# A layer planner's odd steps: one VectorE place, and a second one only when a job took a TensorE place

## The chip, the cores and the metric

The kernel runs on one core of a Trainium2 chip. The metric is the device time of one execution in microseconds. Before the change the median of 3 runs is 6233.53 us (6230.06 to 6236.76). Its engines are named as in the profile: PE (TensorE), PEld (its weight loads), DVE (VectorE), ACT (ScalarE), POOL (GpSimd) and SP (the queue that issues nearly all DMAs).

## What is computed

Two layers on x of shape 4 x 128 x 64 x 64, all in float32. The first is attention over the 4096 positions of an image, with a residual and a normalisation over the channels. The second adds a 3 x 3 convolution, a spectral term (a Fourier transform, a channel mix and its inverse) and a Mamba block, whose core is a scan over the positions.

```python
# layer 0, per image, 4 heads of 32 channels
attn = softmax(einsum('bhnd,bhmd->bhnm', Q, K) * scale)
y    = (einsum('bhnm,bhmd->bhnd', attn, V) merged) @ Wo + bo + x_flat
y    = normalised over channels * gamma + beta
# layer 1
xs   = silu(depthwise causal conv of 4 taps over xi + b)      # 256 channels
dt   = softplus(x_dbl[:8] @ dt_proj + b)
h    = exp(dt*A) * h + dt * B * xs                            # 16 states, 4096 positions
out  = spatial conv + spectral term + out_proj((h.C + xs*D) * silu(z))
```

## The kernel before, in words

The 4096 positions of an image are cut into 8 chunks of 512, so there are 32 chunks. Attention works on a chunk and one of two pairs of heads at a time (a half, H, 64 in all), and in each half walks over 32 tiles of 128 keys. One tile is one **step** t of the main loop (L1019 to the end of the function). So there are 2048 steps of attention, and a chunk of 64 steps. I call the steps 64k to 64k+63 **stretch k** and count the steps in it from 0 to 63.

What a step always issues is written out in the loop, in this order:

- `scores_for_exp` (L472): six matmuls per step into the PSUM tile s2 (L480) and an exponential on ACT into e (L488).
- `scores_for_max` (L424): four matmuls for a tile 39 steps ahead into the PSUM tile s1 (L436), and a maximum on DVE (L443). There is one s1, so the four matmuls of a step wait until the maximum of the step before is done.
- In even steps `scan_state` (L808): a scan on DVE (L817), and on POOL a copy of the state (L826), a product with C (L827) and a sum (L846, for the first state L844). In odd steps `scan_decay` on ACT (L801) and `scan_input_term` on POOL (L806, up to the end of attention).
- a call of `plan.step`, which hands out the step's **places** to jobs.
- `times_values` (L491) for the tile of the step before: four matmuls with V (L500). At the last tile of a half the sum is copied to oz on ACT and DVE (L509, L510).

Everything else is done by **jobs**: Python generators that stop at `yield "PB"`, `yield "D"` and so on, and say by it what they need next: P a place on PE, D on DVE, A on ACT, B one of two PSUM banks, f and x a buffer. `Plan.step` (L122) goes once through the jobs, sorted by rank and due time, and lets each job go on whose needs can be met in this step; each place it uses is gone. A job is let go on once per step, but for P: while its next need is P alone and P places are left, it goes on (L146 to L148). Places left from a step before count for nothing, because L125 sets D, P and A anew. The order of the instructions on every engine thus follows from counts of places and banks alone, with no times in it. During attention, even steps have no place on DVE and PE and one on ACT, odd steps have 2 places on each of the three (L1051 to L1056). Before and after attention a step has 4.

The jobs that ask for DVE places, with the lines of what they do there:

- `scan_input(c, hf)` (L660), one for each half of the 256 channels: the 4 taps of the causal convolution (L674 and three times L679; the sum stands in a bank), then a `sigmoid` (L599): L603, L605 and L608 on ACT, L611 on DVE, L613 on ACT, and a product on POOL (L689).
- when both are done `scan_bc` (L695), and then `scan_dt(c, hf)` (L711): a matmul (L714), ACT work from L722 to L734, with the last (L737) together with L738 on DVE, three products on POOL (L739 to L741), and three steps later, on ACT, a scaling of xs by D (L748) that has to wait until L741 has read xs.
- `gate(c)` (L751): a matmul (L757) and a sigmoid for each half, each ended by a product on POOL (L765).
- `project_kv` (L341), only while a next image's keys are still to be made, that is in stretches 0 to 23 (L350, L355, L356), `project_q` (L405: L412, L417, L418), `output_projection` (L543: L556, L564 to L570, then L587) and `scan_output(c)` (L924): two products on POOL (L938) as soon as the gates of the chunk are there, then four matmul records on PE (L948) that read them, and L954 on DVE.

Also named below: `convolve` (L880, matmuls of 9 taps, L891), `spectral` (L850, its last ACT copy is L874), `flips` (L966), which at the ends of images 0 to 2 gives POOL two further additions (L921, L922) in stretches 8 and 9, 16 and 17, 24 and 25, `normalise` (L512, on POOL L533), and `scan_load` (L779), the DMA of a state's B and C (L784), which has three buffers.

Of the kernel before, what the change touches and what calls it, by code (L numbers as in the profile page):

```python
# [17 lines left out]
P = 128  # L18
# [81 lines left out]
class Plan:  # L100
# [18 lines left out]
    def release(self, bank, steps=1):  # L119
        self.freed.append((self.t + steps, bank))  # L120

    def step(self, t, places):  # L122

        self.t = t
        self.places |= places  # L125
        self.free += [bank for when, bank in self.freed if when <= t]
        self.freed = [e for e in self.freed if e[0] > t]
        for e in sorted((e for e in self.later if e[0] <= t), key=lambda e: e[:3]):
            self.jobs.append((e[1], e[0], e[2], Job(e[3])))
            self.later.remove(e)  # L130
        self.jobs = sorted((j for j in self.jobs if not j[3].done), key=lambda j: j[:3])
        kept = 0
        for *_, job in self.jobs:
            bank = None
            if "B" in job.need and len(self.free) <= kept:
                continue
            if any(c != "B" and not self.places[c] for c in job.need):
                kept += "B" in job.need
                continue
            for c in job.need:  # L140
                if c == "B":
                    bank = self.free.pop(0)
                else:
                    self.places[c] -= 1
            job.advance(bank)
            while not job.done and job.need == "P" and self.places["P"]:  # L146
                self.places["P"] -= 1
                job.advance(None)  # L148
        self.jobs = [j for j in self.jobs if not j[3].done]
# [6 lines left out]
def attention_then_conv_mamba(  # L156
# [43 lines left out]
    for h in range(HEADS):  # L200
        k, j = divmod(h, 2)
        c = COL["bk"] + k
# [9 lines left out]
    for h in range(HEADS):  # L212
        k, j = divmod(h, 2)
        c = COL["bq"] + h
# [112 lines left out]
    plan = Plan(2, {"x": 2, "f": 1})  # L327
# [96 lines left out]
    def scores_for_max(H, s):  # L424

        k = H % PAIRS
        m, t = divmod(s, TPC)
        assert have["K", k, m] == H // PAIRS // NCH
        if s == 0:
            part[H] = att.tile([P, TPC, 2, NCH], F32, tag="part", name=f"part_{H}")  # L430

        tag = "s2" if H == 0 and s % 2 else "s1"
        sc = psum.tile([P, 2, L], F32, tag=tag, name=f"s1_{H}_{s}")
        for n in range(2):
            for j in range(2):
                nc.tensor.matmul(  # L436
                    sc[:, j, :],
                    QT[H][rows[j], n, t * P : (t + 1) * P],
                    KK[k][m][rows[j], :],
                    start=n == 0,  # L440
                    stop=n == 1,
                )
        nc.vector.tensor_reduce(part[H][:, t, :, m], sc, AX.X, ALU.max)  # L443
# [28 lines left out]
    def scores_for_exp(H, m):  # L472

        k = H % PAIRS
        i, t = divmod(m, TPC)
        assert have["K", k, i] == H // PAIRS // NCH
        s = psum.tile([P, 2, L], F32, tag="s2", name=f"s2_{H}_{m}")
        for n, mov in enumerate((QT[H][:, 0, :], QT[H][:, 1, :], MX[H])):
            for j in range(2):
                nc.tensor.matmul(  # L480
                    s[:, j, :],
                    sel[rows[j], :] if n == 2 else KK[k][i][rows[j], t * P : (t + 1) * P],
                    mov[rows[j], :],
                    start=n == 0,
                    stop=n == 2,
                )
        e = att.tile([P, 2, L], F32, tag="e", name=f"e_{H}_{m}", bufs=3)
        nc.scalar.activation(e, s, AF.Exp)  # L488
        es[H, m] = e

    def times_values(H, m):  # L491

        k = H % PAIRS
        i, t = divmod(m, TPC)
        assert have["V", i] == H // PAIRS // NCH
        if m == 0:
            po[H] = psum.tile([P, L], F32, tag="o", name=f"po_{H}")
        e = es.pop((H, m))
        for j in range(2):
            nc.tensor.matmul(  # L500
                po[H][used[j], :],
                VA[i][:, t, 2 * k + j, :],
                e[:, j, :],
                start=m == 0,
                stop=m == NT - 1,
            )
        if m == NT - 1:
            p = po.pop(H)
            nc.scalar.activation(oz[k][used[0], :], p[used[0], :], AF.Identity)  # L509
            nc.vector.tensor_copy(oz[k][used[1], :], p[used[1], :])  # L510
# [284 lines left out]
    def scan_decay(c, v):  # L795
        n, hf = divmod(v, NH)
        k = hf * NS + n

        tag = "o" if plan.t >= HALVES * NT + 2 and v % 2 else "dA"
        dA[c, v] = psum.tile([P, L], F32, tag=tag, name=f"dA_{c}_{k}")  # L800
        nc.scalar.activation(dA[c, v], dts[c][hf], AF.Exp, scale=negA[:, k : k + 1])  # L801

    def scan_input_term(c, v, engine):
        n, hf = divmod(v, NH)
        db[c, v] = loc.tile([P, L], F32, tag="db", name=f"db_{c}_{hf * NS + n}")
        engine.tensor_tensor(db[c, v], us[c][hf], bcs[c, n][0], ALU.mult)  # L806

    def scan_state(c, v):  # L808

        n, hf = divmod(v, NH)  # L810
        k = hf * NS + n
        assert (c, hf) in scaled
        if c >= CHUNKS - 2:
            hs = flat(VA[v % 4])
        else:
            hs = loc.tile([P, L], F32, tag="hs", name=f"hs_{c}_{k}")
        nc.vector.tensor_tensor_scan(  # L817
            hs,
            dA.pop((c, v)),
            db.pop((c, v)),  # L820
            state[:, k : k + 1] if c % NCH else zero,
            ALU.mult,
            ALU.add,
        )
        if c % NCH < NCH - 1:
            nc.gpsimd.tensor_copy(state[:, k : k + 1], hs[:, L - 1 :])  # L826
        nc.gpsimd.tensor_tensor(hs, hs, bcs[c, n][1], ALU.mult)  # L827
        if hf == NH - 1 and (c, n) in taken:
            spare.append((plan.t + 6, taken.pop((c, n))))
        elif hf == NH - 1:  # L830
            ring[0] += 1
        if c >= CHUNKS - 2:

            if v == 0:
                late = psum.tile([P, NH, L], F32, tag=f"s{CHUNKS - c}", name=f"acc_{c}")
                for h in range(NH):
                    accs[c, h] = late[:, h, :]
            if n == 0:
                nc.tensor.matmul(accs[c, hf], ident, xss[c][hf], start=True, stop=False)
            nc.tensor.matmul(accs[c, hf], ident, hs, start=False, stop=n == NS - 1)  # L840
        elif n == 0:
            acc = loc.tile([P, L], F32, tag=f"acc{hf}", name=f"acc_{c}_{hf}")
            accs[c, hf] = acc
            nc.gpsimd.tensor_tensor(acc, xss[c][hf], hs, ALU.add)  # L844
        else:
            nc.gpsimd.tensor_tensor(accs[c, hf], accs[c, hf], hs, ALU.add)  # L846
# [170 lines left out]
    t = 6 - SLOT  # L1017
    loaded = 0
    end = (CHUNKS + 3) * SLOT  # L1019
    while t < end or not plan.idle():  # L1020
        H, m = divmod(t, NT)
        if 0 <= H < HALVES:
            scores_for_exp(H, m)
        h1, s1 = divmod(t + LEAD, NT)
        if 0 <= h1 + 1 < HALVES:
            scores_for_max(h1 + 1, s1)
        H, m = divmod(t - 1, NT)
        last = m == NT - 1
        if last and 0 <= H < HALVES:
            times_values(H, m)  # L1030
        c, s = divmod(t - LAG, SLOT)
        odd = s % 2 == 1
        if -1 <= c < CHUNKS:
            v = c * STATES + s // 2
            if not odd:
                if v >= 0:
                    scan_state(*divmod(v, STATES))
            else:
                if 0 <= v + 1 < CHUNKS * STATES:
                    scan_decay(*divmod(v + 1, STATES))  # L1040
                if 0 <= v + 2 < CHUNKS * STATES:
                    late = t > HALVES * NT
                    scan_input_term(
                        *divmod(v + 2, STATES), nc.vector if late else nc.gpsimd
                    )

                if loaded < CHUNKS * NS and loaded // NS in bcds:
                    if ring[0] or spare[0][0] <= t:
                        scan_load(*divmod(loaded, NS))
                        loaded += 1  # L1050
        if t < -LEAD or t > HALVES * NT:  # L1051
            plan.step(t, {"D": 4, "P": 4, "A": 4})
        elif odd:
            plan.step(t, {"D": 2, "P": 2, "A": 2})
        else:
            plan.step(t, {"D": 0, "P": 0, "A": 1})  # L1056
        if not last and 0 <= H < HALVES:
            times_values(H, m)
        t += 1
# [76 lines left out]
```

## Time and profile before

| | before |
|---|---|
| median of 3 runs | 6233.53 us |
| the profiled execution | 6236.14 us |
| its span (first to last instruction) | 6234.4 us |
| granted TensorE clock, mean | 0.982 |
| start of step 0 | 131.4 us |
| start of the last step, 2047 | 5983.5 us |
| DVE L817, scan, in attention | 832 + 128 times, 1275 ns |
| DVE L679, a tap | 192 times, 738 to 746 ns |
| DVE L674, the first tap | 64 times, 807 ns |
| DVE L611 and L738 | 128 + 64 times, 677 and 678 ns |
| ACT L488, the exponential | 2048 times, 1023 ns |
| POOL L806, L827, L846 | 948, 952 and 900 times, 1281, 1277 and 1279 ns |

A step's four matmul records of L480 with Q and K (8192 in all) give its start in the trace. So the start of every step and the length of every stretch can be read off, and a wait is what a step lasts above another step with the same matmuls. Stretch 12, for example, runs from 2300.07 to 2483.62 us, and stretch 27 from 5063.60 to 5250.67 us. Lines in the profile are those of the kernel before.

### The profile page before, as it was taken

The page shows a single profiled execution, that of the slowest core. Times are in us where ns is not written, and L with a number is a line of the kernel's source. Part 1 is how long each engine was busy: PE and PEld are TensorE (multiplying, and loading weights), DVE is VectorE, ACT ScalarE, POOL GpSimd, SP SyncE. Part 2 cuts the span into 40 slices and gives each one's busy share as a digit, 9 for nine tenths or more (in the row PEclk, how much of TensorE's full clock was granted, in tenths as well). Part 3 has the DMA queues.
Part 4 walks back from the last instruction along what each step waited for, and adds up shares of the span by engine and source line. Part 5 has one row for each costly group of instructions (what it writes and reads, how often), then busy time and mean ns, then how long its engine had stood idle before and what let it go on. Part 6 is the DMA issues. An engine that isn't in the chain of part 4 may idle for free. (4 is left out here: it accounts for less than half of the span.)

```text
span 6234.4 us, 83338 instructions
## 1 busy us (share of the span) xinstructions
PE 6005.2 (96%) x32076; PEld 2540.9 (41%) x32076; DVE 4286.5 (69%) x4406; ACT 3585.0 (58%) x4858; POOL 4579.0 (73%) x4819
## 2 busy tenths in 40 slices
PE   5999999999999999999999999999999999999966
PEld 2444444444444444444444444444444444444321
DVE  4556776777777676777667777776777666767647
ACT  1455666565666555666656566665566556556643
POOL 0005887778887777888787888777788777778877
PEclk7999999999999999999999999999999999999987
DMA  3001222223222222222322221122322211112223
GB/s 111 14 25 47 63 56 61 63 64 98 79 71 60 63 65 60 62 63 73 89 82 65 61 65 60 57 64 67 98 66 71 55 54 54 54 55 58 63 80 85
DMA packets 234624, 404.97 MB, mean 65 GB/s; under 512 B 39272, under 2 KB 40816, under 8 KB 234224
## 3 DMA queue, kind: packets, MB, share of 16 engines
q1 hardware_dynamic: 229840, 397.75, 22.6%
q8 instruction: 251, 4.11, 0.3%
q10 hardware_dynamic: 4384, 1.89, 0.1%
q14 instruction: 149, 1.22, 0.1%
HBM read 350.54 MB, written 49.02 MB: 64 GB/s over the span
## 5 line engine op out<-in xcount | busy, mean ns | idle before, releaser
L443 DVE TENSOR_REDUCE part<-s 128x2 f32<-128x1024 f32 x2048 | 2501.7, 1222 | 1627.4 <-PE s L436 1625.9
L488 ACT ACTIVATE e<-s 128x1024 f32<-128x1024 f32 x2048 | 2095.5, 1023 | 2271.7 <-PE s L480 2263.0
L500 PE MATMUL po<-e,V 128*33 128x512 f32 x8192 | 2160.9, 606 | 2.6 <-DVE oz L510 0.3
L480 PE MATMUL s<-Q,K 64*128 64x512 f32 x8192 | 1504.7, 445 | 22.3 <-ACT e L488 18.5
L436 PE MATMUL s<-K,Q 64*128 64x512 f32 x8192 | 1322.2, 400 | 41.2 <-DVE part L443 39.6
L827 POOL TENSOR_TENSOR hs<-hs,bc 128x512 f32<-128x512 f32 x952 | 1215.5, 1277 | 177.5 <-DVE hs L817 108.6
L480 PEld LDWEIGHTS s<-Q,K 64*128 64x128 f32 x8192 | 610.7, 185 | 1748.9 <-ACT e L488 1179.0
L806 POOL TENSOR_TENSOR db<-u,bc 128x512 f32<-128x512 f32 x948 | 1214.8, 1281 | 0.0
L846 POOL TENSOR_TENSOR acc<-acc,hs 128x512 f32<-128x512 f32 x900 | 1150.9, 1279 | 70.5
L817 DVE TENSOR_TENSOR_SCAN hs<-dA,state,db 128x512 f32<-128x512 f32 x832 | 1060.7, 1275 | 86.0 <-ACT dA L801 54.0
L436 PEld LDWEIGHTS s<-K,Q 64*128 64x128 f32 x8192 | 766.3, 186 | 276.7 <-DVE part L443 99.4
L480 PE MATMUL s<-MX,sel 64*128 64x512 f32 x4096 | 810.9, 392 | 0.0
L826 POOL COPY state<-hs 128x1 f32<-128x1 f32 x864 | 160.2, 185 | 844.8 <-DVE hs L817 844.8
L801 ACT ACTIVATE dA<-dt,negA 128x512 f32<-128x512 f32 x1024 | 702.6, 686 | 116.0 <-DVE hs L817 63.6
L500 PEld LDWEIGHTS po<-e,V 128*33 128x33 f32 x8192 | 299.3, 109 | 913.8 <-issue 879.7
L480 PEld LDWEIGHTS s<-MX,sel 64*128 64x128 f32 x4096 | 384.6, 185 | 92.6
L891 PE MATMUL pf<-xp,cw 128*128 128x512 f32 x576 | 288.2, 617 | 0.0
L452 POOL COPY wide<-mx 128x128 f32<-128x128 f32 x256 | 63.4, 294 | 200.7 <-DVE mx L449 200.7
L817 DVE TENSOR_TENSOR_SCAN hs<-dA,zero,db 128x512 f32<-128x512 f32 x128 | 163.2, 1275 | 7.7 <-POOL db L806 7.4
L840 PE MATMUL acc<-V,cst 128*128 128x512 f32 x128 | 90.1, 807 | 78.2 <-POOL V L827 78.0
L533 POOL TENSOR_TENSOR oz<-oz,rz 128x512 f32<-128x512 f32 x64 | 81.9, 1280 | 107.1 <-DMA rz<-rd 107.1
L891 PEld LDWEIGHTS pf<-xp,cw 128*128 128x128 f32 x576 | 96.2, 188 | 132.4 <-issue 127.4
(144 smaller groups left out, 3847.8 us busy)
## 6 DMA issues: line engine op xcount, KB each, us to landing
bc<-bcd SPq DMA_DIRECT2D x487, 512.0 KB
K<-kd SPq DMA_DIRECT2D x64, 256.0 KB
rz<-rd SPq DMA_DIRECT2D x128, 128.0 KB
K<-bcd SPq DMA_DIRECT2D x42, 256.0 KB
vd<-vst SPq DMA_DIRECT2D x32, 264.0 KB
V<-vd SPq DMA_DIRECT2D x32, 264.0 KB
xq<-in_x SPq DMA_DIRECT2D x32, 256.0 KB
xk<-in_x SPq DMA_DIRECT2D x32, 256.0 KB
```

Source lines behind the costliest of these rows:

```text
L436: nc.tensor.matmul(sc[:, j, :], QT[H][rows[j], n, t * P : (t + 1) * P], KK[k][m][rows[j], :], start=n == 0, stop=n == 1,)
L443: nc.vector.tensor_reduce(part[H][:, t, :, m], sc, AX.X, ALU.max)
L480: nc.tensor.matmul(s[:, j, :], sel[rows[j], :] if n == 2 else KK[k][i][rows[j], t * P : (t + 1) * P], mov[rows[j], :], start=n == 0, stop= ...
L488: nc.scalar.activation(e, s, AF.Exp)
L500: nc.tensor.matmul(po[H][used[j], :], VA[i][:, t, 2 * k + j, :], e[:, j, :], start=m == 0, stop=m == NT - 1,)
L801: nc.scalar.activation(dA[c, v], dts[c][hf], AF.Exp, scale=negA[:, k : k + 1])
L806: engine.tensor_tensor(db[c, v], us[c][hf], bcs[c, n][0], ALU.mult)
L817: nc.vector.tensor_tensor_scan(hs, dA.pop((c, v)), db.pop((c, v)), state[:, k : k + 1] if c % NCH else zero, ALU.mult, ALU.add,)
L826: nc.gpsimd.tensor_copy(state[:, k : k + 1], hs[:, L - 1 :])
L827: nc.gpsimd.tensor_tensor(hs, hs, bcs[c, n][1], ALU.mult)
L846: nc.gpsimd.tensor_tensor(accs[c, hf], accs[c, hf], hs, ALU.add)
L891: nc.tensor.matmul(pf, cw[:, k, :], xps[c][:, dy : dy + RPC, dx : dx + W], start=k == 0, stop=False)
```

## The change

In an odd step of attention there is one place on DVE in place of two. The first job in that step that takes a place on PE by its own turn (not by the inner loop for further P) adds one place on DVE, which jobs that come later in the same pass can take. Places on PE and ACT, even steps, and the steps before and after attention stay as they are. No instruction is added or taken away: jobs only get their places in other steps.

```diff
-    def step(self, t, places):
+    def step(self, t, places, more=False):
         self.t = t
+        self.more = more
         self.places |= places
...
                 else:
                     self.places[c] -= 1
+                    self.places["D"] += (c == "P") * self.more
+                    self.more &= c != "P"
             job.advance(bank)
...
         elif odd:
-            plan.step(t, {"D": 2, "P": 2, "A": 2})
+            plan.step(t, {"D": 1, "P": 2, "A": 2}, more=True)
         else:
             plan.step(t, {"D": 0, "P": 0, "A": 1})
```

## The prediction, made before the changed kernel was run

> **What bounds the kernel now.** I read the page first, then the waits, then stretches of equal content against each other.
>
> ```profile
> PE 6005.2 (96%) x32076; PEld 2540.9 (41%) x32076; DVE 4286.5 (69%) x4406; ACT 3585.0 (58%) x4858; POOL 4579.0 (73%) x4819
> ...
> L443 DVE TENSOR_REDUCE part<-s 128x2 f32<-128x1024 f32 x2048 | 2501.7, 1222 | 1627.4 <-PE s L436 1625.9
> ...
> L436 PE MATMUL s<-K,Q 64*128 64x512 f32 x8192 | 1322.2, 400 | 41.2 <-DVE part L443 39.6
> ```
>
> PE is the bound; its waits for the maximum on DVE are small (41.2 us before L436). But a busy share is a mean. Attention lasts from 131.4 to 5983.5 us. Adding up, step by step, what each step lasts above the quarter-lowest step with the same matmuls gives 119 us of waits in it. They do not lie evenly. Stretches 4 to 23 last 183.6 us nearly all (of it 2.2 us waits), whereas stretch 3 has 7.2 us of waits and stretches 25 to 31 have 7.6, 5.9, four times 7.2 to 7.3, and 8.6. Busy times of whole stretch 12 and its steps 0 to 20, then of stretch 27 and its steps 0 to 20 (columns: window, its length, PE, PEld, DVE, ACT, POOL):
>
> ```profile
> core 0: us, PE busy (x) PEld busy (x) DVE busy (x) ACT busy (x) POOL busy (x), PEclk, DMA share, GB/s
> 2300.07:2483.62 183.55, 182.90 (x1000) 78.14 (x998) 131.48 (x135) 111.44 (x152) 146.79 (x157) 1.00 0.22 61
> 2300.07:2355.59 55.52, 54.91 (x324) 24.43 (x322) 42.31 (x50) 39.31 (x55) 48.95 (x52) 1.00 0.22 62
> 5063.60:5250.67 187.07, 182.53 (x990) 76.17 (x989) 131.16 (x135) 111.45 (x151) 147.16 (x157) 1.00 0.20 55
> 5063.60:5123.06 59.46, 55.54 (x325) 24.26 (x324) 43.59 (x52) 37.44 (x50) 53.80 (x57) 1.00 0.21 59
> ```
>
> Steps 0 to 20 have the same PE jobs in both, but last 59.46 us in stretch 27 against 55.52: 3.94 us more, all of it waiting. The timeline shows a typical cause, at step 6 of stretch 27, where a step loses 1.49 us:
>
> ```profile
> 5079.56 1.28 POOL L741 TENSOR_TENSOR u<-dt,xs 128x512 f32<-128x512 f32 x1
> ...
> 5080.87 0.72 ACT L748 ACTIVATE xs<-xs,vec 128x512 f32<-128x512 f32 x1 [1.19 <-POOL u L741]
> ...
> 5081.50 1.00 ACT L488 ACTIVATE e<-s 128x1024 f32<-128x1024 f32 x1
> ```
>
> In stretches 3 and 26 to 31 both scan_dt halves end in step 1, on the two DVE places of one step. That puts six products (L739 to L741) on POOL at once. ACT's in-order queue then stands before L748 until POOL is through, and the exponential that PE needs stands behind L748. In stretches 4 to 24 the halves end in steps 5 and 11, and L748 does not wait.
>
> [...] A tap (L679) has one tensor in SBUF and one in PSUM; L846 means 1279 ns with such taps beside it. So moving taps should not slow POOL down, and I price that at nothing.
>
> **The change, part by part.** I worked the planner out for both versions; it needs step numbers, places and banks alone, and the built order confirms it. Of the odd steps of attention, 56 have two DVE jobs before, all without a PE job; after, none has. The DVE jobs are 608 in both.
>
> *The direct part* is small. The waits of the 54 such steps with a measured successor sum to 15.0 us in the two steps behind them, but nearly all of this is in stretches 3 and 25 to 31, where it is counted below. In stretches 4 to 23 the one pair (step 37: L611 and a tap) shows no wait over 0.04 us.
>
> *Stretches 4 to 23*: five steps differ. Taps go from steps 37, 39, 41 to 39, 41, 43, all beside a PE job; L603 and L605 go from 42 and 43 to 44 and 45, and L874 from 43 to 42. DVE has 0.9 to 2.4 us idle before L443 there, and a tap is 0.74. ACT gets 0.62 us more in steps 44 and 45, and before the exponentials of steps 45 and 46 it now waits for PE:
>
> ```profile
> 2422.92 1.02 ACT L488 ACTIVATE e<-s 128x1024 f32<-128x1024 f32 x1 [1.33 <-PE s L480]
> ...
> 2426.39 1.02 ACT L488 ACTIVATE e<-s 128x1024 f32<-128x1024 f32 x1 [1.26 <-PE s L480]
> ```
>
> Both waits are longer than 0.62, so the cover holds: 0. Stretch 1 has a similar tap with `project_kv` in step 43 and 0.08 us of wait; from below nothing can be won. I take 0.05 each, +1.0 us for the 20.
>
> *Stretch 3* becomes the same as 4 to 23, with the same number of PE steps: 7.2 - 2.2 = 5.0 us less.
>
> *Stretches 27 to 30*. Their head becomes that of stretch 12 (scan_dt ends in steps 5 and 11, one gate in 9), and L757 goes from step 7 to step 55 of the stretch before. But one thing differs from stretch 12: there `scan_output` has its PE place in step 31, here still in step 21, because its gates are done early. Its L948 waits for two L938 on POOL. In stretch 12 POOL has no gap from step 5 to step 24; it ends the second L844 at 57.14 us from the stretch's start. The two L938 (1.28 and 1.26, 2.48 with overlap) would follow it: 59.62. PE gets to step 21 at 55.52, less the 1.06 us of the L757 that stretch 12 has in step 17: 54.46. It needs the second product 2.24 us later (in stretch 27 L948 could start 1.37 into the step, and its first pair takes 0.87), at 56.70, so PE will wait 2.9 us there. In stretch 27 before, the second L938 ends at 61.95 (5125.55 - 5063.60) and PE waits 0.33. So the time to that point falls by 61.95 - 59.62 = 2.33 us and not by the 3.94 of the head: POOL keeps the rest. Stretch 25 shows that such a wait is real:
>
> ```profile
> 4750.30 2.48 POOL L938 TENSOR_TENSOR acc<-acc,zg 128x512 f32<-128x512 f32 x2
> 4751.61 0.30 PEld L948 LDWEIGHTS py<-acc,outw 128*128 128x128 f32 x2 [2.60 <-POOL acc L938]
> ```
>
> The moved L757 costs 0.86 us in step 55 (a step with two such jobs lasts 4.26, with one 3.40). Later waits (steps 22 to 40) fall from 1.48 to 0.75, as in stretch 24, which has no project_kv either: -0.7. Sum: -2.33 + 0.86 - 0.7 = -2.2 each, -8.7 for four.
>
> *Stretch 26*: POOL has no L826 up to step 17, as in stretches 10 and 18, where L844 ends at 55.66. 55.66 + 2.48 = 58.14 against 60.56 before; -2.42 + 0.86 - 0.7 = -2.3. *Stretch 25*: flips give POOL 3.0 us more; as in stretches 9 and 17 L844 would end at 58.75, L938 at 61.23, against 61.18 before. +0.05 + 0.86 - 0.7 = +0.2. *Stretch 24*: a wait of 0.42 in step 49 goes, and one step less has a PE job (0.2): -0.6. *Stretch 31*: 59.62 against 61.92, and some 0.3 of later DVE waits: -2.6. *Stretches 1 and 2*: one more step with a PE job each (+0.2 each), a wait of 0.75 in step 34 of stretch 2 goes, one of 0.75 in step 2 comes: +0.2 in all.
>
> *SP's queue*: the loads L784 are built in the same steps but for three of chunk 0, which come 6 steps later and are still 19 steps ahead of their use. The write L707 comes four steps later in stretches 25 to 30, long before step 6 of the next stretch, where its first load stands: 0. *The tail* (250.9 us from the last step on) has the same steps from 2056 on; scan_dt of chunk 30 is two steps later at its start. POOL has a run without gaps there up to L533 at 6008.9, and the same work in it: 0, with 3 us either way.
>
> Sum: 1.0 - 5.0 - 8.7 - 2.3 + 0.2 - 0.6 - 2.6 + 0.2 = -17.8 us. From the span of 6234.4 that gives 6216.6; the profiled execution (6236.14) is 2.61 above the median, so I take the difference from the median: 6233.53 - 17.8 = 6215.7.
>
> **The rivals.**
>
> *POOL keeps everything.* If in stretches 25 to 31 the second L938 ends no earlier than before, those seven only pay 0.86 and win 0.7: +1.1. With stretch 3 and 24 (-5.6), the others and +1.0 the sum is -3.3: 6230.2. For it: POOL is 90% busy in steps 0 to 20 of stretch 27 (53.80 of 59.46). Against: it has gaps there of 1.48 and 1.76 us, and one L765 less to do.
>
> *The wait at step 21 does not come.* POOL may be ahead by then. Then 2.9 us fall away in stretches 27 to 30, 1.4 in 26, 2.6 in 25 and 3.9 in 31, 19.5 in all: 6196.2, the lowest bound; half of it would give 6206. Against: stretch 12 has no gap in POOL to take up.
>
> *ACT becomes late (slower).* In stretches 4 to 23 L603 and L605 now stand in front of khi (L355) and the exponentials of steps 45 and 46; klo (L356) on DVE waits for khi, and the scan and maximum wait behind klo. If ACT's slack is not there, each stretch pays two ACT operations and a decay, 0.62 + 0.62 + 0.69 = 1.93 us: 20 x 1.93 = 38.6, so +20.8: 6254.3. It decides where ACT's idle time before L488 in step 46 is under 0.6; it is 1.26 before.
>
> That the change does not do what it says is ruled out by the built order (56 to 0).
>
> **How the numbers follow.** Forecast 0.62 (from -12 to -27), POOL keeps everything 0.17, no wait at step 21 0.12, ACT late 0.09. A measurement of this kernel can tell about 0.2% from no change, 12.5 us: faster means below 6221.0. Faster: 0.60 + 0.12 = 0.72. Within: 0.02 + 0.17 = 0.19. Slower: 0.09. The range goes from 6204, halfway into the second rival, to 6231, just past the first one.
>
> **What would show it.** Right: stretches 25 to 30 with L748 not waiting for L741, PE L948 waiting about 2.9 us for L938 in step 21 of stretches 27 to 30 and about 4 in 31; stretch 3 near 183.6 us; 4 to 23 unchanged within 0.1. Wrong: a longer stretch 12, with waits at steps 44 to 46; a second L938 at or above 61.9 us in stretch 27; a tail over 254 us.

## The result, and the profile after

The median of 14 runs after is 6221.72 us (6215.94 to 6231.35), beside 6233.66 us before (14 runs): 11.9 us less, a ratio of 0.9982 with a 95% interval from 0.9974 to 0.9991. Forecast was 17.8 less: the median lies in the range that was given (6204 to 6231), but a hair outside the -12 to -27 that the forecast itself covers. The profiled execution took 6228.18 us (span 6226.4, mean clock 0.982), so it is 6.5 above the median of its kernel. Lines of the kernel after are four higher in the loop: L443 is L447, L436 is L440, L480 is L484, L714 is L718, L748 is L752, L844 is L848, L938 is L942, L948 is L952.

The page of after, the same three rows as shown of before:

```profile
PE 6006.5 (96%) x32076; PEld 2549.8 (41%) x32076; DVE 4299.9 (69%) x4406; ACT 3573.0 (57%) x4858; POOL 4578.5 (74%) x4819
...
L447 DVE TENSOR_REDUCE part<-s 128x2 f32<-128x1024 f32 x2048 | 2501.9, 1222 | 1636.5 <-PE s L440 1634.6
...
L440 PE MATMUL s<-K,Q 64*128 64x512 f32 x8192 | 1321.6, 400 | 34.9 <-DVE part L447 33.4
```

The busy times hardly say anything. The windows by stretch of after say more: stretch 3, stretch 12 and its steps 0 to 20, stretch 27 and its steps 0 to 20.

```profile
core 0: us, PE busy (x) PEld busy (x) DVE busy (x) ACT busy (x) POOL busy (x), PEclk, DMA share, GB/s
637.82:821.54 183.72, 183.01 (x1000) 78.25 (x998) 131.75 (x135) 111.35 (x152) 147.07 (x158) 1.00 0.23 61
2294.81:2478.51 183.70, 183.03 (x1001) 78.23 (x999) 131.67 (x135) 111.35 (x152) 146.79 (x157) 1.00 0.22 61
2294.81:2350.39 55.58, 54.97 (x324) 24.43 (x322) 42.37 (x50) 39.30 (x55) 49.01 (x52) 1.00 0.22 62
5056.69:5242.35 185.66, 182.03 (x990) 76.75 (x988) 131.92 (x134) 110.16 (x150) 148.02 (x158) 1.00 0.20 56
5056.69:5111.22 54.53, 53.93 (x324) 24.13 (x322) 43.41 (x50) 37.96 (x52) 48.28 (x53) 1.00 0.23 63
```

Stretch 3 now lasts what stretch 12 lasts. The head of stretch 27 takes 54.53 us, against 59.46 before and 54.46 in the forecast. But the whole stretch is only 1.4 shorter (185.66 against 187.07), and stretches 28 to 30 are 0.5 to 0.8 us *longer* than before. Here is step 21 of stretch 27 in the timeline of after:

```profile
5112.49 1.26 POOL L848 TENSOR_TENSOR acc<-xs,hs 128x512 f32<-128x512 f32 x1
5113.72 2.48 POOL L942 TENSOR_TENSOR acc<-acc,zg 128x512 f32<-128x512 f32 x2
5115.03 0.30 PEld L952 LDWEIGHTS py<-acc,outw 128*128 128x128 f32 x2 [2.81 <-POOL acc L942]
```

The second product ends at 5116.20, that is 59.51 after the start of the stretch (forecast 59.62), and the step waits 2.82 us (forecast 2.9). So this came as it was worked out. What did not is in the clock. Pieces of the trace of after, 3.41 us each, called **windows** from here on: three in a row around step 21 of stretch 27, two around step 21 of stretch 28, and two around the end of stretch 27 (PEclk is the column after POOL):

```profile
5110.82:5114.23 3.41, 1.84 (x14) 0.86 (x10) 3.11 (x3) 1.74 (x3) 3.25 (x5) 1.00 0.12 42
5114.23:5117.65 3.42, 2.53 (x6) 0.74 (x8) 0.00 (x0) 0.00 (x0) 3.34 (x5) 1.00 0.44 111
5117.65:5121.06 3.41, 3.41 (x22) 1.40 (x20) 1.30 (x2) 1.03 (x1) 3.33 (x4) 1.00 0.00 0
5298.56:5301.97 3.41, 1.07 (x8) 0.36 (x4) 1.78 (x2) 1.61 (x2) 3.33 (x4) 1.00 0.44 104
5301.97:5305.38 3.41, 3.41 (x6) 0.70 (x6) 0.00 (x0) 0.00 (x0) 3.25 (x5) 0.50 0.27 50
5237.12:5240.53 3.41, 3.41 (x18) 1.55 (x17) 2.81 (x3) 2.02 (x3) 1.55 (x3) 1.00 0.00 0
5240.53:5243.94 3.41, 3.41 (x13) 1.46 (x14) 0.00 (x0) 0.00 (x0) 2.38 (x2) 0.50 0.46 125
```

In attention the granted clock in this trace falls to 0.50 thirteen times, each time for 3.41 us; I call one such time a **halving**. The starts of four of them, 5240.53, 5301.97, 5428.26 and 5489.70 us, are 18, 37 and 18 times 3.4133 us apart, so I count windows of 3.4133 us from these starts. The wait of stretch 27 lies across the start of a window: PE is busy for 1.84 and 2.53 us in the two, and the clock behind each is 1.00. In stretch 28 the wait falls into one window, PE is busy for 1.07 of 3.41 us, and the next window has a clock of 0.50. The second kind has no idle time at all (3.41 of 3.41 us busy from 5237.12 on); what this window holds and most others do not is L718, whose matmuls use 8 rows:

```profile
5238.59 1.98 PE L718 MATMUL pdt<-xd,dtw 8*128 8x512 f32 x4
5240.50 1.92 PE L504 MATMUL po<-e,V 128*33 128x512 f32 x4
5242.35 1.22 PE L484 MATMUL s<-Q,K 64*128 64x512 f32 x4
```

Four matmuls of L504 take 1.92 us here and 1.05 at a clock of 1.00. Before, the L714 of the two halves stood in different steps (53 and 55) in the late stretches; after, both stand in step 63, as they do ahead of stretch 12.

The halving behind step 21 of stretch 28 costs 1.22 us (the step lasts 8.35 us, and 7.13 in the same stretch without one, in a run below), that in steps 63 and 0 costs 0.87 + 0.71 = 1.58 (5.14 against 4.27, and 3.06 against 2.35). The price is not always the same: in the kernel with the late part alone, below, two others behind step 21 cost 1.71 and 1.06 (stretches of 186.46 and 185.81 us against 184.75). Attention has 5 halvings before, all in steps 63 and 0, and 13 after: nine of that kind and one behind step 21 in each of stretches 28 to 31. At these prices that is an estimated 5 x 1.58 = 7.9 us against 9 x 1.58 + 4 x 1.22 = 19.1. In stretches 28 to 31 they come one after the other: with two halvings stretches 28 to 30 last 187.53, 187.69 and 187.80 us, about 55.0 windows, so that the next step 21 stands nearly in the same place of its window.

In the kernel with 40 rows, below, half the clock also follows a window in which PE is busy for 1.61 of 3.41 us, and so idle for 1.8:

```profile
5657.65:5661.06 3.41, 1.61 (x3) 0.60 (x4) 0.56 (x1) 0.52 (x1) 3.41 (x4) 1.00 0.50 153
5661.06:5664.47 3.41, 3.41 (x8) 0.67 (x8) 0.00 (x0) 0.00 (x0) 3.25 (x4) 0.50 0.00 1
```

### The profile page after: what moved, and what is told of

The parts are those of the page before. It is cut to its first block, busy times and chain, and to the rows that moved or that the text cites. A ratio compares the mean times of both kernels' runs of the same rounds, so it can differ in the third digit from the quotient of the medians.

```text
span 6226.4 us, 83392 instructions
## 1 busy us (share of the span) xinstructions
PE 6006.5 (96%) x32076; PEld 2549.8 (41%) x32076; DVE 4299.9 (69%) x4406; ACT 3573.0 (57%) x4858; POOL 4578.5 (74%) x4819
## 3 DMA queue, kind: packets, MB, share of 16 engines
q1 hardware_dynamic: 229840, 397.75, 22.9%
q14 instruction: 150, 1.22, 0.1%
## 5 line engine op out<-in xcount | busy, mean ns | idle before, releaser
L447 DVE TENSOR_REDUCE part<-s 128x2 f32<-128x1024 f32 x2048 | 2501.9, 1222 | 1636.5 <-PE s L440 1634.6
L504 PE MATMUL po<-e,V 128*33 128x512 f32 x8192 | 2166.8, 607 | 2.8 <-DVE oz L514 0.3
L484 PE MATMUL s<-Q,K 64*128 64x512 f32 x8192 | 1507.5, 446 | 6.3 <-ACT e L492 2.5
L440 PE MATMUL s<-K,Q 64*128 64x512 f32 x8192 | 1321.6, 400 | 34.9 <-DVE part L447 33.4
L484 PEld LDWEIGHTS s<-Q,K 64*128 64x128 f32 x8192 | 612.2, 185 | 1737.2 <-ACT e L492 1174.2
L850 POOL TENSOR_TENSOR acc<-acc,hs 128x512 f32<-128x512 f32 x900 | 1150.9, 1279 | 70.6
L440 PEld LDWEIGHTS s<-K,Q 64*128 64x128 f32 x8192 | 769.8, 187 | 262.3 <-DVE part L447 82.9
L484 PE MATMUL s<-MX,sel 64*128 64x512 f32 x4096 | 812.1, 393 | 0.0
L504 PEld LDWEIGHTS po<-e,V 128*33 128x33 f32 x8192 | 300.0, 109 | 916.8 <-issue 881.9
L484 PEld LDWEIGHTS s<-MX,sel 64*128 64x128 f32 x4096 | 385.3, 185 | 92.4
L844 PE MATMUL acc<-V,cst 128*128 128x512 f32 x128 | 88.4, 794 | 80.5 <-POOL V L831 80.4
```

Of the source, the lines that this page charges most:

```text
L440: nc.tensor.matmul(sc[:, j, :], QT[H][rows[j], n, t * P : (t + 1) * P], KK[k][m][rows[j], :], start=n == 0, stop=n == 1,)
L484: nc.tensor.matmul(s[:, j, :], sel[rows[j], :] if n == 2 else KK[k][i][rows[j], t * P : (t + 1) * P], mov[rows[j], :], start=n == 0, stop= ...
L504: nc.tensor.matmul(po[H][used[j], :], VA[i][:, t, 2 * k + j, :], e[:, j, :], start=m == 0, stop=m == NT - 1,)
```

## The experiments

**The early and the late part alone.** The change up to stretch 23, and from stretch 24 on; the rest keeps two places.

```diff
-        elif odd:
+        elif odd and t < 24 * SLOT:
             plan.step(t, {"D": 1, "P": 2, "A": 2}, more=True)
+        elif odd:
+            plan.step(t, {"D": 2, "P": 2, "A": 2})
```

The late one has `t >= 24 * SLOT` instead.

> The change up to stretch 23 alone; from stretch 24 on the places are those of before. My sum gives -5.0 for stretch 3, +0.2 for 1 and 2 and +0.1 to 0.2 for each of 4 to 23 (measured in the trace of after): -2 to -4 us against before, some 6230 to 6232. Rival (ACT or DVE is late in the steady stretches in most runs): above 6234.

> The change from stretch 24 on alone. Theory 1 (heads gain what was worked out, and part is given back by stretches of 3.41 us at half TensorE clock that follow the wait at step 21 and the two scan_dt matmul pairs of step 63): -8 us, 6226, with such half-clock stretches in stretches 27 to 31 at steps 21 and 63. By my working without them: -14, 6220. If the waits on POOL alone had grown: no half-clock stretches in 27 to 31, and L938 later than 59.6 us after the start of its stretch.

Measured: the early part 6228.06 us, ratio 0.9990 (0.9983 to 0.9997), the late one 6227.85, ratio 0.9992 (0.9983 to 1.0000). Against 6233.57 that is -5.5 and -5.7, and together nearly the -11.9 of after. The early part gives more than the 2 to 4 that were expected; in its trace stretch 3 is 4.90 shorter, and the tail 1.4. The late part gives less than 8, and of the halvings expected at steps 21 and 63 of stretches 27 to 31 only three came, all behind step 21. This kernel shows the same stretch with and without halvings. Stretches 27 and 28 happen to have none, and both are 2.31 us shorter than before; 29 and 30, with one behind each step 21, are only 0.67 and 1.23 shorter. Stretch 28 and its steps 0 to 20 in the late kernel:

```profile
5243.35:5428.10 184.75, 181.06 (x990) 76.64 (x989) 130.83 (x134) 110.22 (x150) 146.91 (x156) 1.00 0.21 55
5243.35:5297.86 54.51, 53.90 (x322) 24.14 (x320) 42.34 (x50) 37.97 (x52) 47.94 (x52) 1.00 0.21 63
```

187.06 before, 184.75 here, 187.53 after: the same order of instructions, and of the last two the first has a granted clock of 1.00 throughout, the second 0.50 for 6.6 us, or two halvings. At the prices above they come to an estimated 1.22 + 1.58 = 2.80 us; the difference is 2.78.

**Without the wait at step 21.** `scan_output` eight steps later in stretches 25 to 31 (line of after), on top of after and on top of before.

```diff
-        plan.at((c + 1) * SLOT + LAG + 2, 0, scan_output(c))
+        plan.at((c + 1) * SLOT + LAG + (10 if 22 <= c < 29 else 2), 0, scan_output(c))
```

> After, but scan_output of chunks 22 to 28 is due 8 steps later, so that its PE place is step 31 in stretches 25 to 31 as in 4 to 24. Theory 1: the waits at step 21 (1.5 to 4.8 us, 24 us in all in the profiled run of after) go, with the half-clock stretches behind them; nothing takes their place, because POOL has caught up by step 31: 6196 to 6204. Rival (POOL is the bound over the whole stretch, the wait only moves to step 31 or to the scans): 6216 to 6224.

> Before with only scan_output of chunks 22 to 28 due 8 steps later. By the built order its PE jobs push scan_dt apart in stretches 26 to 31 too (ends in steps 3 and 7), so the burst on POOL and the wait at step 21 both go without the change: the heads are as in stretch 25 of before (3.3 us of waits), nothing waits at 21: -3 to -4.5 us for each of stretches 25 to 31: 6204 to 6214. If the gain of e3_scanout needs the change: 6225 or more.

Measured: on top of after 6198.80 us, ratio 0.9943 (0.9931 to 0.9956), which is 22.9 below after. The wait is gone and so is each halving behind step 21. The group of L952, after and then this kernel:

```profile
L952 PE MATMUL py<-acc,outw 128*128 128x512 f32 x128 | 69.3, 663 | 17.2 <-POOL acc L942 16.0 <-DVE acc L939 0.9
```

```profile
L952 PE MATMUL py<-acc,outw 128*128 128x512 f32 x128 | 63.2, 616 | 0.9 <-DVE acc L939 0.9
```

The 16.0 us of waits for POOL are gone, and the mean of one falls from 663 to 616 ns: the longest took 1184 ns in after, and takes 697 here. On top of before the edit gives 6207.84, ratio 0.9958 (0.9945 to 0.9970). So the change is worth 9.0 us where scan_output is later (8.2 if each is set against the runs of before taken beside it), 4.9 of it in stretch 3.

**Without the 8-row matmuls.** L714 multiplies all 40 rows of xd, with weights of zero for the 32 that it does not want; the product is the same.

```diff
-    dtw = const.tile([DTR, DI], F32, name="dtw")
-    nc.scalar.dma_start(dtw, dt_w)
+    dtw = const.tile([DTR + 2 * NS, DI], F32, name="dtw")
+    nc.vector.memset(dtw, 0.0)
+    nc.scalar.dma_start(dtw[:DTR, :], dt_w)
...
-            pdt, dtw[:, hf * P : (hf + 1) * P], xd[:DTR, :], start=True, stop=True
+            pdt, dtw[:, hf * P : (hf + 1) * P], xd, start=True, stop=True
```

> After, but the two scan_dt matmuls (L714 before) contract 40 rows in place of 8: the 32 further rows of the weight are zero, so the result is the same. Theory 1a (the half-clock stretch after step 63 follows from few rows in use): such stretches at steps 63 and 0 become rarer, from 9 in the profiled run of after to under 3, each worth 1.6 us: 6208 to 6216. Theory 1b (it is the time in which TensorE does little, not the rows; or it is chance): unchanged, 6219 to 6225, with some 9 of them.

> Before with 40 rows in the two scan_dt matmuls, to see the change without the half-clock stretches of step 63: the 5 in attention go and the steps of L714 last 0.2 us less: 6217 to 6224. Against e4_rows40 (6209.8) the change would then be worth -8 to -14: my -17.8, plus 0.5 for each of five stretches whose wait at step 34 stayed, plus 1.3 for each half-clock stretch behind step 21. If the half-clock stretches are chance: 6230 to 6236.

Measured: on top of after 6209.81 us, ratio 0.9959 (0.9947 to 0.9972); on top of before 6221.64, ratio 0.9980 (0.9972 to 0.9987). So with 40 rows on both sides the change is worth 11.8 us (11.0 against the runs of before taken beside each). In both traces no halving is left in steps 63 and 0; those behind step 21 remain, six with the change (stretches 25 and 27 to 31; after has four) and one without (stretch 25). The end of stretch 27 in after with 40 rows (lines one higher again):

```profile
5226.16 1.88 PE L719 MATMUL pdt<-xd,dtw 40*128 40x512 f32 x4
5227.97 1.05 PE L505 MATMUL po<-e,V 128*33 128x512 f32 x4
5228.95 0.73 PE L485 MATMUL s<-Q,K 64*128 64x512 f32 x4
```

1.88 us where the 8 rows took 1.98, and the four matmuls behind it take 1.05 us where they took 1.92. Not only the late stretches win: on top of before, stretches 4 to 23 are 10.3 us shorter, of it an estimated 5 x 1.58 = 7.9 by the halvings that they lose.

**The same wait, but PE works in it.** On top of the 40 rows, PE multiplies const weights twice into the bank that L952 then overwrites, in the step 21 in question.

```diff
+        for _ in range(2 if c in (22, 24, 25, 26, 27, 28) else 0):
+            nc.tensor.matmul(pf, outw[:, 0, :], inw, start=True, stop=True)
```

> The change with the 40-row L714, and in step 21 of stretches 25 and 27 to 31 PE multiplies two weight tiles (128x128 by 128x512, about 0.87 us each) into the same bank first; the matmuls of L948 then overwrite that. Nothing else moves. With the 40-row L714 alone the median was 6209.81 and the clock was halved for 3.41 us behind step 21 in all six of these stretches. Theory (little PE work in a 3.41 us window halves the clock in the next one): PE still cannot go on before the second L938, which ends at 59.5 us after the start of the stretch as before, but the wait is half filled, no window is nearly empty, none of the six halvings comes, and each stretch is some 1.3 to 1.5 us shorter: 8 to 9 us less, 6201 to 6202. Rival (the wait itself costs the time, and the halved clock in the trace is only a sign of it, or the halving comes from the product's arrival): no change or slower by up to 1.7 us per stretch, 6209 to 6220.

Measured: 6201.49 us (6199.73 to 6204.81), ratio 0.9949 (0.9936 to 0.9963), 8.3 below the same kernel without the filler. Step 21 of stretch 28 (L951 is the filler, L943 the products, L955 the matmuls that wait):

```profile
5284.43 1.98 PE L951 MATMUL py<-inw,outw 128*128 128x512 f32 x4
5285.61 2.48 POOL L943 TENSOR_TENSOR acc<-acc,zg 128x512 f32<-128x512 f32 x2
5286.92 2.35 PE L955 MATMUL py<-acc,outw 128*128 128x512 f32 x4 [0.51 <-POOL acc L943]
5289.20 1.05 PE L505 MATMUL po<-e,V 128*33 128x512 f32 x4
```

Step 22 starts 61.66 us after the start of the stretch, as in the late kernel without a halving (5304.99 - 5243.35 = 61.64). The step is as long as it is without a halving (7.13 us), although PE has 1.98 us more to do in it, and the kernel is faster: no window of attention has half the clock. PE is busy for 6.53 of the 7.13 us of the step, and the second product still ends 59.57 us after the start of the stretch (59.51 in stretch 27 of after). So half the clock went with PE's idle time in these six steps, and not with the wait for POOL as such.

**Both edits together**, on top of after and on top of before.

> After with both edits: scan_output of chunks 22 to 28 due 8 steps later, and 40 rows in the two scan_dt matmuls. If the two causes of half-clock stretches are these and independent, none is left in attention: the 4 of e3_scanout (1.6 us each) go and L714's steps last 0.2 us less, as in e4_rows40: 6184 to 6192. If such stretches come by chance: 4 or more stay, 6196 to 6200.

> The kernel before with both other edits (the 40-row L714, and scan_output 8 steps later in stretches 25 to 31), so that it stands to the kernel with all three as before stands to after, with nearly no halved clock on either side. With each edit alone it was 6221.64 and 6207.84 (12.0 and 26.6 us less than before); with all three 6186.37. Theory (the change is worth a sum near the forecast, without halvings): at most one halved window in attention, the median at 6234.4 - 12.0 - 26.6 = 6195.8, and so the change worth about 9 us on top, half of it from stretch 3. Rival (the other two edits already take what the change gives in stretches 25 to 31): the median is at 6191.5 or below, and only the 5 us of stretch 3 are left.

Measured: on top of after 6186.37 us (6185.47 to 6191.57), ratio 0.9925 (0.9912 to 0.9939); this is the fastest kernel here. On top of before 6194.89 (6194.72 to 6196.35), ratio 0.9939 (0.9926 to 0.9951). Neither has a halving in attention. The change is worth 8.5 us between the two. In the two traces, whose spans differ by 9.6, it is 4.9 in stretch 3, 3.3 in stretches 27 to 30 and 1.9 in 24 to 26 and 31, and the lead-in, the tail and the other stretches come to -0.5. The rival, that only stretch 3 is left, falls.

**The burst on POOL by itself.** In the kernel before, the products L739 to L741 of the second half go to DVE in chunks 24 to 29, so that POOL gets three at once and not six.

```diff
-        nc.gpsimd.tensor_tensor(e, w, e, ALU.subtract)
+        eng = nc.vector if hf and 24 <= c < 30 else nc.gpsimd
+        eng.tensor_tensor(e, w, e, ALU.subtract)
```

and the same for the other two.

> Before, but the three products behind L738 of the second half (L739 to L741) run on VectorE for chunks 24 to 29, that is in stretches 26 to 31. If the six products at once on POOL are what holds L748 and with it PE at step 6 of these stretches, the 1.5 us there fall under 0.5 and L748 does not wait for L741; in their place DVE has 2.1 us more in step 1, with a wait of 1 to 2 us in steps 2 to 4: 6222 to 6234 in all. If the wait has another cause, step 6 still loses 1.5 us.

Measured: 6257.82 us (6253.22 to 6260.96), ratio 1.0037 (1.0024 to 1.0051), slower, which was not expected. The waits at which it was aimed did go: steps 6, 8 and 10 of stretch 27 waited 1.49, 0.74 and 0.94 us and now 0.20, 0.00 and 0.12. But step 3 lasts 8.10 us where it lasted 2.35. Steps 2 and 3 of stretch 28 in this kernel (lines one higher than before from L739 on):

```profile
5262.89 1.29 DVE L740 TENSOR_TENSOR spe<-u,spe 128x512 f32<-128x512 f32 x1
5263.58 1.73 POOL L807 TENSOR_TENSOR db<-u,bc 128x512 f32<-128x512 f32 x1
...
5264.21 1.65 DVE L741 TENSOR_TENSOR dt<-dt,spe 128x512 f32<-128x512 f32 x1
...
5265.27 1.71 POOL L740 TENSOR_TENSOR spe<-u,spe 128x512 f32<-128x512 f32 x1
5265.89 1.64 DVE L742 TENSOR_TENSOR u<-dt,xs 128x512 f32<-128x512 f32 x1
...
5267.45 1.21 DVE L443 TENSOR_REDUCE part<-s 128x2 f32<-128x1024 f32 x1
...
5268.72 1.22 PE L436 MATMUL s<-K,Q 64*128 64x512 f32 x4 [4.13 <-DVE part L443]
```

The three products stand in DVE's queue ahead of the maximum L443, 4.6 us long, and PE waits for it (4.13 us before L436); then half the clock follows (L436 takes 1.22 us where 0.73 is usual). Beside these products POOL's instructions last longer too: L807 takes 1.73 us here and its L740 1.71, where their medians in this kernel are 1.28. Beside the taps they do not, which is what the prediction priced at nothing: in the trace of before the 49 L846 that a tap overlaps by more than 0.4 us take 1279 ns on average, and so do the 770 that no tap overlaps. What makes the difference was not shown.

**One place, and no second one.** In the traces, two jobs that ask for a DVE place work between one scan and the next 54 times in attention before, and never after. So the place that a job on PE adds is never used by a second job, and all of this is the effect of one place in place of two.

## Why the prediction was right, and where not

Differences from before by part, in us. The last column is the kernel with 40 rows and the filler against before with 40 rows, that is, the change with the halvings taken away on both sides, but for one (about 1.1) in stretch 25 of the latter.

| part | forecast | after | without halvings |
|---|---|---|---|
| stretches 0 to 2 | +0.2 | -0.5 | -0.1 |
| stretch 3 | -5.0 | -4.9 | -4.9 |
| 4 to 23 | +1.0 | +0.2 | +0.2 |
| 24 | -0.6 | +1.2 | -0.4 |
| 25 | +0.2 | +0.2 | -0.8 |
| 26 | -2.3 | -2.3 | -2.3 |
| 27 to 30 | -8.7 | +0.4 | -8.3 |
| 31 | -2.6 | -0.2 | -2.3 |
| attention | -17.8 | -5.9 | -18.9 |

- *The sum as worked out holds where the clock holds.* The last column gives -18.9, or about -17.8 without the halving in stretch 25. That it meets the forecast so closely is luck in part: the parts are off by up to 0.8 us, and the errors cancel. Stretch 3 became a stretch like 4 to 23, and these did not change.
- *The step that failed* is the pricing of a moved or a waiting step by its matmuls alone: "PE will wait 2.9 us there" was taken to cost 2.9 us, and L714 in step 63 was not priced at all. Both were followed by half the clock in after: the waits of stretches 28 to 31, which left PE busy for 0.60 to 1.07 us of a 3.41 us window, and nine of the 30 steps that hold both pairs of L718. Neither the forecast nor a rival has a term for the clock, so that the median still fell into the range owes something to the range's width. After has eight halvings more than before, an estimated 11.2 us in the profiled execution: -5.9 - 11.2 = -17.1. The lead-in and the tail give -0.8 and -1.3, so the profiled span is 8.0 less. Of the other runs only the mean granted clock is on record: 0.9823 on average over the 14 runs of after, 0.9838 over 61 runs of before taken beside the experiments. A halving is 3.41 us at 0.50 and so takes 1.71 us of clock; the difference is an estimated five halvings more in a run of after, against eight in the profiled one, if the time at half the clock in the lead-in and the tail is alike on average (209 us before and 186 after in the two profiled executions). Fewer halvings fit medians that lie further apart (11.9) than the profiled spans (8.0).
- *Stretches 27 to 30.* The time to the second L938 fell by 61.95 - 59.51 = 2.44 (forecast 2.33). "Later waits, -0.7" was mis-sized: step 34 still waits 0.74, and only 0.17 in step 35 went. "The moved L757 costs 0.86" was mis-sized as well: the steps from 43 on, whose PE jobs are dealt out otherwise, together take 0.3 more in the late kernel. The two errors cancel: +0.1 against +0.16.
- *POOL keeps everything* falls with the 59.51; *the wait at step 21 does not come* falls with the 2.82; *ACT becomes late* falls with the +0.2 of twenty stretches.
- L752 does not wait for L745 in stretches 26 to 31, and the steps 6, 8 and 10 of stretch 27, which lasted 3.83, 3.09 and 3.28 us, last 2.39, 2.40 and 2.47. The burst experiment agrees that this wait made them long, but does not prove it by itself: POOL also had the 5.8 us of step 3 to catch up. The tail is 249.6 us, inside the 3 us given to it.

## What to carry to other kernels

Where PE is the bound, look at the granted clock behind each remaining wait and behind matmuls on few rows, not only at the wait: here a wait that left PE 1.07 of 3.41 us to do was paid a second time, by 1.22 us (1.06 and 1.71 in two stretches of the late kernel). Filling six such waits with matmuls whose result is overwritten took 8.3 us off the median, and widening L714 with zeros cost no time (a median of 588 ns each with 40 rows; 587 before and 588 after with 8). And a job moved off a busy engine must be costed on the queue that it joins: three products took 4.6 us of DVE ahead of the one instruction that PE waits for.

## What the runs showed of the hardware

Not expected was half the clock behind windows in which PE is busy throughout but that hold matmuls on 8 rows. In the traces of before and after, 53 steps (23 and 30) hold the L714 of both halves. The first matmul of 14 of them (5 and 9) starts 0.04 to 0.36 or 1.33 to 1.50 us into its window, and the next window has a clock of 0.50; the 39 others start elsewhere, and the clock behind them is 1.00. In the traces of the five kernels with 40 rows (before, after, both edits on either, filler) 17 of 131 such steps start in those two ranges, and no halving follows; so the halvings did not go because the steps moved to other places of their windows. Why these two ranges count, and what happens between 8 and 40 rows, was not shown.

Of the idle kind, in the traces of before and after half the clock follows the four windows of attention at the full clock in which PE is busy least: 0.60, 0.94, 1.06 and 1.07 of 3.41 us, all in after. The next is the one with 1.84 us in stretch 27 of after, and the clock behind it is 1.00. With 40 rows the window with 1.61 us, shown above, is followed by 0.50. Nothing here shows what lies between 1.61 and 1.84 us.
